# A graph convolution whose pools are opened once, and whose table is loaded or made in parts between the first block's products

## The chip, the core and the metric

The kernel runs on one core of a Trainium2 chip. The metric is the device time of one execution in microseconds (us). The five engines each work through a queue of their own in order: PE (TensorE, matrix products), DVE (VectorE), ACT (ScalarE), POOL (GpSimd, which here only issues the row gathers) and SP (SyncE, which issues nearly all other transfers). They meet through semaphores. SBUF is the working memory on the chip, with 128 partitions, and PSUM is where matrix products land. DRAM stands for the memory outside the core's SBUF and PSUM.

## What is computed

A graph of 12,500 nodes with 128 features and 200,000 edges, sorted by destination, goes through an attention layer (the first half of the time, which the change leaves alone) and then through three graph convolutions with batch norm. The part that matters:

```python
def _gcn_conv(x, W, b, src, dst, norm, num_nodes):
    h = x @ W
    msg = h[src] * norm[:, None]
    out = jax.ops.segment_sum(msg, dst, num_segments=num_nodes)
    return out + b
def _batch_norm(x, gamma, beta):
    mean = jnp.mean(x, axis=0)
    var = jnp.mean((x - mean) ** 2, axis=0)
    return (x - mean) * jax.lax.rsqrt(var + EPS) * gamma + beta
...
src, dst, norm = _gcn_norm(edge_index, n)        # dinv[src] * dinv[dst], with self loops
h = _gcn_conv(x, W1, b1, src, dst, norm, n)      # 128 -> 256
h = _batch_norm(jax.nn.relu(h), g1, beta1)
h = _gcn_conv(h, W2, b2, src, dst, norm, n)      # 256 -> 128
h = _batch_norm(jax.nn.relu(h), g2, beta2)
h = _gcn_conv(h, W3, b3, src, dst, norm, n)      # 128 -> 128
return _batch_norm(h, g3, beta3)
```

## The kernel before

**The data of a convolution.** A convolution sums, for each destination node, rows of a table `t_d[i]` (12,544 rows of 128 floats in DRAM, already scaled by `dinv`). The same table stands in SBUF as `hs`, 98 slices of 128 rows (6.4 MB). The destinations are cut into 106 tiles of `TN` = 118 nodes. An edge can go two ways. For each pair of a tile and a slice there are 13 slots, so most edges are served by a matrix product that picks rows out of `hs`. The others, at most 768 a tile, are gathered row by row from `t_d[i]` by POOL.

**`take(b, m)`** (L1211 to L1229) serves block `b`, which is nine tiles; there are 12 blocks. It goes through the 98 slices in seven parts of `SG` = 14 slices. For each part it loads the indices `gi` (L1215), VectorE turns them into a one-hot `go` (L1221, four slices at a time), PE multiplies it with the slices of `hs` (L1224), ScalarE copies the product to `stage` (L1226), and two transfers store it to a block `m` in DRAM (L1228).

**`reduce(b, m)`** (L1231) takes the tiles of a block one by one. Each needs the block's `m` complete: it is read back in another order as `mr` (L1245), and a tile has 20 matmul instructions over `mr` (L1253) and 12 over the gathered `rows` (L1255). The gathers of a tile are six POOL instructions on line 148 (the helper `gather`), into the pool `ga` with five buffers. `finish` (L1150) begins a tile with its own rows `tg` (L1154, L1159) and ends three tiles with the scaling by `dinv` (L1163) and the function `use`.

**The order.** The parts of `take(b)` and the tiles of `reduce(b - 1)` alternate, so block 0 is taken alone, and the last block, with seven tiles, is reduced alone. After the last tile the statistics of the batch norm (L1275, L1280) give a scale and a shift; `affine` (L1277) and `through` (L1288) put them into the next weights. Then `transform` (L1301) makes the next table: groups of `NG` = 4 slices, on PE (L1312), two passes on VectorE (L1315, L1316, the latter writing `hs`), and a store to `t_d[i]` (L1318). For the second convolution it also loads half of the features, `hb`, from DRAM (L1307). The first convolution finds its table in `t_d[0]` and loads `hs` in one transfer:

```python
                nc.sync.dma_start(hs, rows_of(t_d[0], 0, NS))            # L1324
                ...
                conv(t_d[0], use1)
                sr = s.enter_context(tc.tile_pool(name="sr", bufs=3))
                ps = s.enter_context(tc.tile_pool(name="ps", bufs=2, space=PSUM))
                ...
                transform(sr, ps, [hb_d], wa, row, t_d[1])
```

After the third convolution an output loop loads `x1` (L1376), multiplies by the scale (L1381), adds (L1384, L1388) and stores (L1389), four slices at a time.

**Pools.** `conv_slots` opens its pools anew for each convolution and closes them at its end. `sr` (three buffers of each of its tiles: `hb`, `og`, `x1`, `yg`) and a PSUM pool for `transform` are opened after that. The order of instructions within each engine's queue isn't the order of the program text: a scheduler in the framework sorts them at build time, by the program's order and by when it reckons an instruction can start. It tracks which parts of a tile or a table an instruction reads and writes. `conv_rows` stands beside `conv_slots` for graphs with too many gathered edges a tile; this input takes `conv_slots`.

Of the kernel before, what the change touches and what calls it, by code (L numbers as in the profile page):

```python
# [8 lines left out]
FP = mybir.dt.float32  # L9
BF = mybir.dt.bfloat16  # L10
# [7 lines left out]
P = 128  # L18
D = 128
# [29 lines left out]
def tile_gnn(ctx: ExitStack, tc: tile.TileContext, x, src, dst, ea, wqkvT, weT, w1, w2, w3, par, out):  # L49
# [26 lines left out]
    def groups(n, g):  # L76
        return [(a, min(g, n - a)) for a in range(0, n, g)]
# [580 lines left out]
    def fast():  # L658
# [505 lines left out]
                                    op=ALU.mult)  # L1164
            use(wk, t0, n, zt[:, :n * TN], ps)

        def conv_rows(table, use):

            with ExitStack() as s:
                ew = s.enter_context(tc.tile_pool(name="ew", bufs=1))  # L1170
                srcA = ew.tile([P, NTT, JJ], I32, name="srcA")
                dlA = ew.tile([P, NTT, JJ], BF, name="dlA")
                nc.sync.dma_start(srcA, sw_d.rearrange("t (p j) -> p t j", j=JJ))
                nc.sync.dma_start(dlA, dlb_d.rearrange("t (p j) -> p t j", j=JJ))
                ga = s.enter_context(tc.tile_pool(name="ga", bufs=3))
                wk = s.enter_context(tc.tile_pool(name="wk", bufs=2))
                ps = s.enter_context(tc.tile_pool(name="ps", bufs=2, space=PSUM))
                for t0, n in groups(NTT, GN):
                    zp = ps.tile([P, GN, TN], FP, name="zp")

                    def add(i):
                        rows = ga.tile([P, JJ, D], FP, name="rows")
                        for j in range(JJ):
                            gather(rows[:, j, :], table, srcA[:, t0 + i, j:j + 1])
                        oh = wk.tile([P, JJ, TN], FP, name="oh")
                        one_hot(oh, dlA[:, t0 + i, :])
                        for j in range(JJ):
                            nc.tensor.matmul(zp[:, i, :], rows[:, j, :], oh[:, j, :], start=False, stop=(j == JJ - 1))

                    for _ in finish(wk, table, t0, n, zp, use, ps, add):  # L1190
                        pass

        def conv_slots(table, use):

            with ExitStack() as s:
                tb = s.enter_context(tc.tile_pool(name="tb", bufs=1, space=PSUM))
                nums = tb.tile([P, TN], FP, name="nums")
                nc.vector.tensor_copy(nums, iota_f[:, :TN])  # L1200
                blocks = s.enter_context(tc.tile_pool(name="blocks", bufs=3, space=DRAM))
                gy = s.enter_context(tc.tile_pool(name="gy", bufs=3))
                gx = s.enter_context(tc.tile_pool(name="gx", bufs=3))
                sg = s.enter_context(tc.tile_pool(name="sg", bufs=2))
                mt = s.enter_context(tc.tile_pool(name="mt", bufs=3))
                ga = s.enter_context(tc.tile_pool(name="ga", bufs=5))
                wk = s.enter_context(tc.tile_pool(name="wk", bufs=2))
                ps = s.enter_context(tc.tile_pool(name="ps", bufs=2, space=PSUM))
                TS = TB * SB

                def take(b, m):  # L1211
                    for g in range(NS // SG):
                        stage = sg.tile([TS, SG, D], FP, name="stage")
                        gi = gy.tile([P, TB, SG * SB], U8, name="gi")
                        nc.sync.dma_start(gi.rearrange("p t k -> p (t k)"),  # L1215
                                          gi_d[b, g].rearrange("t k -> (t k)").unsqueeze(0)
                                          .to_broadcast([P, TS * SG]))
                        gv = gi.rearrange("p t (s k) -> p s t k", k=SB)
                        for a, n in groups(SG, 4):
                            go = gx.tile([P, 4, TB, SB], FP, name="go")  # L1220
                            nc.vector.tensor_scalar(go[:, :n], gv[:, a:a + n], iota_q, None, op0=ALU.is_equal)  # L1221
                            gp = ps.tile([TS, 4, D], FP, name="gp")
                            for i in range(n):
                                nc.tensor.matmul(gp[:, i, :], go[:, i].rearrange("p t k -> p (t k)"),  # L1224
                                                 hs[:, g * SG + a + i, :], start=True, stop=True)
                            nc.scalar.copy(stage[:, a:a + n, :], gp[:, :n, :])  # L1226
                        for x, y in ((0, 112), (112, TS)):
                            nc.sync.dma_start(m[x:y, g * SG:(g + 1) * SG, :], stage[x:y])  # L1228
                        yield  # L1229
# [31 lines left out]
                for b in range(NBK + 1):  # L1261
# [8 lines left out]
                    for _ in tiles:  # L1270
                        pass

        def stats(st, h, t0, n):
            w = min(n * TN, N - t0 * TN)
            nc.vector.bn_stats(st[:, t0 // GN, :], h[:, :w])  # L1275
# [11 lines left out]

        def through(pool, ps, abs_, ws):  # L1288

            br = ps.tile([P, D], FP, name="br")  # L1290
            wa = []
            for k, (ab, w) in enumerate(zip(abs_, ws)):
                wk_ = pool.tile([P, D], FP, name=f"wa{k}")
# [4 lines left out]
            nc.vector.tensor_copy(row, br)  # L1298
            return wa, row

        def transform(sr, ps, more, wa, row, table):  # L1301

            for s0, n in groups(NS, NG):
                parts = [big[:, s0 * P:(s0 + n) * P]]
                for h in more:
                    hb = sr.tile([P, NG * P], FP, name="hb")
                    nc.sync.dma_start(hb[:, :n * P], h[:, s0 * P:(s0 + n) * P])  # L1307
                    parts.append(hb)
                tp = ps.tile([P, NG, D], FP, name="tp")
                for i in range(n):  # L1310
                    for k, (h, w) in enumerate(zip(parts, wa)):
                        nc.tensor.matmul(tp[:, i, :], h[:, i * P:(i + 1) * P], w, start=(k == 0),  # L1312
# [6 lines left out]

        def convolutions(conv):  # L1320
            with ExitStack() as s:
                once = s.enter_context(tc.tile_pool(name="once", bufs=1))
                st = [once.tile([P, NST, 6], FP, name=f"st{k}") for k in range(2)]
                nc.sync.dma_start(hs, rows_of(t_d[0], 0, NS))  # L1324

                def use1(wk, t0, n, zt, ps):
                    a, b = t0 * TN, (t0 + n) * TN
                    hx = wk.tile([P, GN * TN], FP, name="hx")
                    for k, h in enumerate((big[:, a:b], hx[:, :b - a])):
                        hq = ps.tile([P, GN * TN], FP, name="hq")  # L1330
                        nc.tensor.matmul(hq[:, :n * TN], w1s[:, k * D:(k + 1) * D], zt, start=True, stop=True)
                        nc.scalar.activation(h, hq[:, :n * TN], AF.Relu, bias=pars[:, k:k + 1])
                        stats(st[k], h, t0, n)
                    nc.sync.dma_start(hb_d[:, a:b], hx[:, :b - a])

                conv(t_d[0], use1)
                sr = s.enter_context(tc.tile_pool(name="sr", bufs=3))
                ps = s.enter_context(tc.tile_pool(name="ps", bufs=2, space=PSUM))
                abs_ = [affine(once, st[k], pars[:, 2 + k:3 + k], pars[:, 4 + k:5 + k], k) for k in range(2)]
                wa, row = through(once, ps, abs_, [w2s[:, k] for k in range(2)])  # L1340
                transform(sr, ps, [hb_d], wa, row, t_d[1])

            with ExitStack() as s:
                once = s.enter_context(tc.tile_pool(name="once", bufs=1))
                st = once.tile([P, NST, 6], FP, name="st")

                def use2(wk, t0, n, zt, ps):
                    h = big[:, t0 * TN:(t0 + n) * TN]
                    nc.scalar.activation(h, zt, AF.Relu, bias=pars[:, 6:7])
                    stats(st, h, t0, n)  # L1350

                conv(t_d[1], use2)
                sr = s.enter_context(tc.tile_pool(name="sr", bufs=3))
                ps = s.enter_context(tc.tile_pool(name="ps", bufs=2, space=PSUM))
                ab = affine(once, st, pars[:, 7:8], pars[:, 8:9], 0)
                wa, row = through(once, ps, [ab], [w3s])
                transform(sr, ps, [], wa, row, t_d[2])

            with ExitStack() as s:
                once = s.enter_context(tc.tile_pool(name="once", bufs=1))  # L1360
                st = once.tile([P, NST, 6], FP, name="st")

                def use3(wk, t0, n, zt, ps):
                    h = big[:, t0 * TN:(t0 + n) * TN]
                    nc.scalar.activation(h, zt, AF.Identity, bias=pars[:, 9:10])
                    stats(st, h, t0, n)

                conv(t_d[2], use3)
                sr = s.enter_context(tc.tile_pool(name="sr", bufs=3))
                ps = s.enter_context(tc.tile_pool(name="ps", bufs=2, space=PSUM))  # L1370
                ab = affine(once, st, pars[:, 10:11], pars[:, 11:12], 0)
                wa, row = through(once, ps, [ab], [ident])
                for s0, n in groups(NS, NG):
                    full = min(n, N // P - s0)
# [1 line left out]
                    nc.sync.dma_start(x1[:, :full, :], rows_of(x1_d, s0, full))  # L1376
                    if full < n:
                        nc.sync.dma_start(x1[:N % P, full, :], x1_d[(s0 + full) * P:N, :])
                    yp = ps.tile([P, NG, D], FP, name="yp")
                    for i in range(n):  # L1380
                        nc.tensor.matmul(yp[:, i, :], big[:, (s0 + i) * P:(s0 + i + 1) * P], wa[0], start=True, stop=True)  # L1381
                    for r, m in ((P, slice(0, full)), (N % P, slice(full, n))):
# [67 lines left out]
```

## Time and profile before

| | |
|---|---|
| median of 3 runs | 7293.77 us (7284.83 to 7306.85) |
| the profiled execution | 6154.56 us, of which its span 6152.8 us |
| mean granted TensorE clock in it | 0.796 of full speed |
| busy: PE, DVE, ACT, POOL | 4406.0, 3396.2, 1011.7, 4084.2 us |
| attention layer and preparation | 0 to 2970 us |
| three convolutions | 2970 to 6093 us |
| output loop | 6093 to 6153 us |

The median and the profiled execution are different executions of the same kernel, and the profiled one is 1139 us shorter. Durations below are those of the profiled one. In the profile's rows, "L1224 PE MATMUL gp<-hs,go x7056" is the group of matmul instructions of line 1224 that read `hs` and `go` and write `gp`; each product of float32 data is two matmul instructions. PEld is the load of the stationary operand, which overlaps PE. SPq is SP's queue of transfers. In the timeline a row gives the start, the duration, the engine, the line, and in brackets how long the engine had been idle and what it waited for last; rows of equal instructions that follow each other are merged.

### The profile page before, as it was taken

How to read it: one execution, taken by the hardware profiler on the slowest of the kernel's cores; microseconds unless marked ns; L12 is line 12 of the kernel's file. 1: busy time of each engine (PE TensorE's matmuls, PEld its weight loads, DVE VectorE, ACT ScalarE, POOL GpSimd, SP SyncE). 2: the span in 40 equal slices, each digit the busy share in tenths (PEclk: the TensorE clock that was granted, in tenths of full speed). 3: DMA queues.
4: the chain of work that ended last, by engine and by line, in shares of the span. 5: the costliest groups of instructions: out<-in, count | busy, mean ns of one | idle time of the engine just before them, and what ended most of it. 6: DMA issues, size and time to landing. Idle time of an engine off the chain costs nothing. (4 is left out here: it accounts for less than half of the span.)

```text
span 6152.8 us, 80384 instructions
## 1 busy us (share of the span) xinstructions
PE 4406.0 (72%) x28564; PEld 4115.5 (67%) x28564; DVE 3396.2 (55%) x5972; ACT 1011.7 (16%) x2374; POOL 4084.2 (66%) x3617
## 2 busy tenths in 40 slices
PE   6676666666666665767487787877787787778777
PEld 2666655555566665666377777777777776777777
DVE  7566688887876677655243343353343344434344
ACT  3111111110111111111112122111121211112120
POOL 0777788888888888777266566636666664666663
PEclk9677766666676776767788888898888888888888
DMA  6555544433444444454588888878888887888888
GB/s 188 152 143 138 137 112 106 113 103 109 105 128 120 122 112 112 131 132 114 150 214 216 218 216 218 213 209 217 219 216 221 213 211 204 219 219 219 221 215 209
DMA packets 607714, 1051.07 MB, mean 171 GB/s; under 512 B 191227, under 2 KB 418491, under 8 KB 607201
## 3 DMA queue, kind: packets, MB, share of 16 engines
q1 hardware_dynamic: 464311, 695.85, 41.5%
q0 software_dynamic: 142608, 348.39, 23.9%
q8 instruction: 232, 3.80, 0.3%
q14 instruction: 175, 1.43, 0.1%
q10 hardware_dynamic: 388, 1.60, 0.1%
HBM read 773.19 MB, written 272.26 MB: 170 GB/s over the span
## 5 line engine op out<-in xcount | busy, mean ns | idle before, releaser
L148 POOL DMA_INDIRECT rows<-t_d,srcO x1908 | 1827.6, 958 | 1329.2 <-issue 560.2
L148 POOL DMA_INDIRECT kv<-kv_d,srcA x1696 | 2252.3, 1328 | 536.7 <-issue 484.3
L1249 DVE TENSOR_TENSOR oh<-nums,dlS 128x1888 f32<-128x1888 f32 x318 | 674.3, 2121 | 1527.2 <-PE zp L1255 1517.9
L1253 PE MATMUL zp<-oh,mr 128*128 128x118 f32 x6360 | 966.6, 319 | 567.5 <-DMA mr<-m 440.4
L1253 PEld LDWEIGHTS zp<-oh,mr 128*128 128x128 f32 x6360 | 925.5, 233 | 586.4 <-DMA mr<-m 348.7
L1019 PE MATMUL qe<-qt,oht 128*128 128x128 f32 x3392 | 841.4, 415 | 247.3 <-DVE kv L1020 110.7
L1224 PE MATMUL gp<-hs,go 128*117 128x128 f32 x7056 | 891.8, 281 | 125.8 <-DVE go L1221 69.8
L1019 PEld LDWEIGHTS qe<-qt,oht 128*128 128x128 f32 x3392 | 767.1, 310 | 289.7 <-issue 166.8
L1224 PEld LDWEIGHTS gp<-hs,go 128*117 128x117 f32 x7056 | 831.9, 184 | 165.1 <-issue 117.1
L1226 ACT COPY stage<-gp 117x512 f32<-117x512 f32 x1008 | 521.8, 532 | 1375.0 <-PE gp L1224 936.8
L1020 DVE TENSOR_TENSOR kv<-qe,kv 128x512 f32<-128x512 f32 x424 | 289.4, 685 | 678.8 <-DMA kv<-kv_d,srcA 536.8
L1089 PE MATMUL acc<-vals,oh 128*118 128x137 f32 x3392 | 539.8, 329 | 150.5 <-DVE vals L1082 150.0
L1089 PEld LDWEIGHTS acc<-vals,oh 128*118 128x118 f32 x3392 | 522.1, 225 | 171.6 <-DVE vals L1082 171.3
L1221 DVE TENSOR_SCALAR go<-gi,iota_q 128x468 f32<-128x468 uint8 x1008 | 427.8, 456 | 224.5 <-DMA gi<-gi_d 111.8
L1255 PE MATMUL zp<-oh,rows 128*128 128x118 f32 x3816 | 513.2, 288 | 0.2 <-DMA rows<-t_d,srcO 0.2
L1255 PEld LDWEIGHTS zp<-oh,rows 128*128 128x128 f32 x3816 | 492.2, 206 | 0.4 <-DMA rows<-t_d,srcO 0.4
L1058 PE MATMUL ends<-ident,mg 128*8 128x128 f32 x212 | 53.0, 343 | 344.4 <-DVE mg L1053 305.6
L1082 DVE TENSOR_TENSOR vals<-kv,vals 128x2048 f32<-128x2048 f32 x106 | 242.3, 2286 | 27.2 <-ACT vals L1081 26.8
L1058 PEld LDWEIGHTS ends<-ident,mg 128*8 128x8 f32 x212 | 11.7, 96 | 366.1 <-DVE mg L1053 298.8
L1023 DVE TENSOR_REDUCE sc<-kv 128x128 f32<-128x2048 f32 x106 | 240.8, 2272 | 0.0
L677 DVE TENSOR_TENSOR oh<-iota_f,dlA 128x1888 f32<-128x1888 f32 x106 | 224.0, 2113 | 5.0 <-PE acc L1089 5.0
L1036 PE MATMUL sm<-wbd,et 128*128 128x32 f32 x848 | 167.8, 351 | 45.0 <-DVE mg L1075 37.7
(242 smaller groups left out, 3648.1 us busy)
## 6 DMA issues: line engine op xcount, KB each, us to landing
m<-stage SPq DMA_DIRECT2D x252, 784.0 KB
mr<-m SPq DMA_DIRECT2D x318, 560.0 KB
dw_b<-dlb_d SPq DMA_DIRECT2D x106, 512.0 KB
gi<-gi_d SPq DMA_DIRECT2D x252, 204.8 KB
rows<-t_d,srcO POOLq DMA_INDIRECT x1908
kv<-kv_d,srcA POOLq DMA_INDIRECT x1696
ebx<-in_edge_attr_dram SPq DMA_DIRECT2D x106, 256.0 KB
mr<-m SPq DMA_DIRECT2D x318, 75.0 KB
```

The lines of the kernel that those rows point to most:

```text
L148: nc.gpsimd.indirect_dma_start(out=o, out_offset=None, in_=table[:, :], in_offset=bass.IndirectOffsetOnAxis(ap=idx, axis=0))
L1019: nc.tensor.matmul(qe[:, k, :], ohv[:, :, j + k], qt, start=True, stop=True)
L1020: nc.vector.tensor_tensor(qk[:, j:j + 4, :], qe, qk[:, j:j + 4, :], op=ALU.mult)
L1023: nc.vector.tensor_reduce(sc.rearrange("p h j -> p j h"), qk.rearrange("p j (h c) -> p j h c", h=H), AX.X, ALU.add)
L1082: nc.vector.tensor_tensor(vh[:, :, :, :C], kv[:, :, D:].rearrange("p j (h c) -> p j h c", h=H), vh[:, :, :, C:].to_broadcast([P, JJ, H, C] ...
L1089: nc.tensor.matmul(acc, oh[:, j, :], va[:, j, :], start=(j == 0), stop=(j == JJ - 1))
L1221: nc.vector.tensor_scalar(go[:, :n], gv[:, a:a + n], iota_q, None, op0=ALU.is_equal)
L1224: nc.tensor.matmul(gp[:, i, :], go[:, i].rearrange("p t k -> p (t k)"), hs[:, g * SG + a + i, :], start=True, stop=True)
L1226: nc.scalar.copy(stage[:, a:a + n, :], gp[:, :n, :])
L1249: nc.vector.tensor_tensor(oh, nums.unsqueeze(1).to_broadcast(sh), dlS[:, t, :].unsqueeze(2).to_broadcast(sh), op=ALU.is_equal)
L1253: nc.tensor.matmul(zp[:, i, :], mr[:q, j, :], oh[:q, j, :], start=False, stop=False)
L1255: nc.tensor.matmul(zp[:, i, :], rows[:, j, :], oh[:, RC + j, :], start=False, stop=(j == JO - 1))
```

## The change

The pools of a convolution are opened once for all three, by `conv_slots(s)`, which returns the PSUM pool and a function `run(table, use, ready)`. Before the products of part `g` in block 0, `take` now calls `ready(g)`. In the first convolution `ready` is `load`, one of seven loads of `hs`; in the second and third it is `transform` for the 14 slices of the part, in groups of 4, 4, 4 and 2. All products that go through PSUM outside `take` and `reduce` share one name, `bank`. `ga` has four buffers instead of five, and `sr`, now open throughout, two instead of three. `nums` is filled once. The core of the diff:

```diff
+        def pools(s, *names):
+            return [s.enter_context(tc.tile_pool(name=n, bufs=b)) for n, b in names]
+
+        def bank(ps):
+            return ps.tile([P, NG * D], FP, name="bank")
...
-        def conv_slots(table, use):
-            with ExitStack() as s:
-                tb = s.enter_context(tc.tile_pool(name="tb", bufs=1, space=PSUM))
-                nums = tb.tile([P, TN], FP, name="nums")
-                nc.vector.tensor_copy(nums, iota_f[:, :TN])
-                blocks = s.enter_context(tc.tile_pool(name="blocks", bufs=3, space=DRAM))
-                gy = s.enter_context(tc.tile_pool(name="gy", bufs=3))
...
-                ga = s.enter_context(tc.tile_pool(name="ga", bufs=5))
...
+        def conv_slots(s):
+            gy, gx, sg, mt, ga, wk = pools(s, ("gy", 3), ("gx", 3), ("sg", 2), ("mt", 3), ("ga", 4), ("wk", 2))
+            blocks = s.enter_context(tc.tile_pool(name="blocks", bufs=3, space=DRAM))
+            tb = s.enter_context(tc.tile_pool(name="tb", bufs=1, space=PSUM))
+            ps = s.enter_context(tc.tile_pool(name="ps", bufs=2, space=PSUM))
+            nums = tb.tile([P, TN], FP, name="nums")
+            nc.vector.tensor_copy(nums, iota_f[:, :TN])
+            TS = TB * SB
+
+            def run(table, use, ready):
                 def take(b, m):
                     for g in range(NS // SG):
+                        if b == 0:
+                            ready(g)
                         stage = sg.tile([TS, SG, D], FP, name="stage")
...
+            return ps, run
+
...
-        def transform(sr, ps, more, wa, row, table):
-
-            for s0, n in groups(NS, NG):
+        def transform(sr, ps, more, wa, row, table, g):
+
+
+            for s0, n in [(g * SG + a, n) for a, n in groups(SG, NG)]:
...
         def convolutions(conv):
             with ExitStack() as s:
-                once = s.enter_context(tc.tile_pool(name="once", bufs=1))
+                once, sr = pools(s, ("once", 1), ("sr", 2))
+                ps, run = conv(s)
                 st = [once.tile([P, NST, 6], FP, name=f"st{k}") for k in range(2)]
-                nc.sync.dma_start(hs, rows_of(t_d[0], 0, NS))
+
+                def load(g):
+                    nc.sync.dma_start(hs[:, g * SG:(g + 1) * SG, :], rows_of(t_d[0], g * SG, SG))
...
+                run(t_d[0], use1, load)
                 abs_ = [affine(once, st[k], pars[:, 2 + k:3 + k], pars[:, 4 + k:5 + k], k) for k in range(2)]
                 wa, row = through(once, ps, abs_, [w2s[:, k] for k in range(2)])
-                transform(sr, ps, [hb_d], wa, row, t_d[1])
...
+                run(t_d[1], then(AF.Relu, 6), lambda g: transform(sr, ps, [hb_d], wa, row, t_d[1], g))
+                ab = affine(once, st[0], pars[:, 7:8], pars[:, 8:9], 0)
+                wa3, row3 = through(once, ps, [ab], [w3s])
+                run(t_d[2], then(AF.Identity, 9), lambda g: transform(sr, ps, [], wa3, row3, t_d[2], g))
+                ab = affine(once, st[0], pars[:, 10:11], pars[:, 11:12], 0)
                 wa, row = through(once, ps, [ab], [ident])
```

`then(func, b)` is the old `use2` and `use3` in one function.

## The prediction

> **What bounds the kernel now.** I read the time of each stretch first, because the change touches only the three graph convolutions and mainly their starts. The stretches below are cut at the first product over the exchanged blocks (L1253) and at the end of each convolution; columns are length, busy time and instruction count of each engine, granted clock, DMA share and GB/s.
>
> ```profile
> core 0: us, PE busy (x) PEld busy (x) DVE busy (x) ACT busy (x) POOL busy (x), PEclk, DMA share, GB/s
> 2970.00:3066.00 96.00, 38.13 (x255) 35.84 (x256) 19.80 (x40) 17.50 (x35) 28.50 (x30) 0.68 0.83 201
> 3066.00:4030.00 964.00, 768.41 (x5847) 740.82 (x5845) 388.32 (x512) 194.16 (x374) 579.27 (x606) 0.88 0.81 215
> 4030.00:4145.00 115.00, 84.15 (x652) 80.66 (x653) 60.24 (x114) 18.05 (x37) 29.25 (x30) 0.88 0.75 218
> 4145.00:5072.00 927.00, 735.39 (x5703) 718.73 (x5701) 367.29 (x474) 173.85 (x338) 580.50 (x606) 0.89 0.84 216
> 5072.00:5168.00 96.00, 63.58 (x451) 59.09 (x452) 53.32 (x103) 17.85 (x36) 29.27 (x30) 0.84 0.68 201
> ...
> 6093.00:6153.00 60.00, 33.30 (x199) 30.06 (x198) 37.08 (x66) 0.59 (x2) 0.00 (x0) 0.81 0.71 202
> ```
>
> The long stretches are set by PE (80%) together with DMA (81 to 84%). The three starts, 96 + 115 + 96 = 307 us, are where no engine and no transfer is full: PE is busy 40 to 73%. The last 60 us are the output. The timeline shows what the starts are made of.
>
> ```profile
> 2972.42 5.96 SPq L1324 DMA_DIRECT2D hs<-t_d  x1
> 2978.43 24.46 SPq L1215 DMA_DIRECT2D gi<-gi_d  x3
> 3007.92 3.74 PE L1224 MATMUL gp<-hs,go 128*117 128x128 f32 x16 [49.90 <-DMA tg<-t_d]
> ...
> 4115.97 5.04 PE L1224 MATMUL gp<-hs,go 128*117 128x128 f32 x28 [8.41 <-DVE go L1221]
> ...
> 4121.19 3.42 PE L1224 MATMUL gp<-hs,go 128*117 128x128 f32 x28 [0.18 <-ACT stage L1226]
> ```
>
> The load of the whole table (6.4 MB) is issued at 2972.4, and the first product runs 35 us later. In the other starts the new table is made first, and then block 0 is taken with waits of 8.4 us for its indices, after which 28 matmuls take 5.0 instead of 3.4 us.
>
> ```profile
> 6102.77 0.50 SPq L1376 DMA_DIRECT2D x<-x_d  x1
> ...
> 6105.85 0.69 DVE L1384 TENSOR_TENSOR x<-x,row 128x512 f32<-128x512 f32 x1 [2.11 <-DMA x<-x_d]
> ```
>
> In the output VectorE waits for a load issued 3.1 us earlier: with three buffers this loop is limited by latency.
>
> **The first convolution's start.** One load becomes seven, each before the part that reads it. Part 0 with its indices is 0.92 + 0.2 MB; at the 288 to 291 GB/s of the windows from 2980 to 3010 that is 3.9 us, and with 3 us to land the first product comes near 2980, 28 us sooner. It can't all be kept, as the bytes remain: up to the first block product the queues move the table 6.4, nine index loads 1.8, nine stores of `m` 7.4, four tiles of gathers 1.6 and about 1 of `tg` and `db`, 18.2 MB, or 63 us at 290 GB/s, against 93.7 us now (2972.4 to 3066.1). So between -31 and -10 (if the index waits stay and the stores queue behind the loads): I take -23. Here a rule speaks against the change: the Trainium skill (DMA: Bandwidth & Descriptors, section Bandwidth) wants transfers of 1 MiB or more for 75% of peak, and each part is 0.92 MB. By the rule the load would lose a quarter, 22 us becoming 29, and the saving 7. But in the row nearest, the 256 KB loads and stores of the transform (4040 to 4080), the queues moved 262 to 279 GB/s, 4 to 9% below the large load: 1 to 2 us. I go by the row.
>
> **The second start.** It is counted from the end of the batch-norm constants (4035.5) to the first block product (4145.1): 109.6 us. The transform's work is not removed but put between the parts. Per part it has 14 x 4 matmul instructions of 0.11 us, 6.2 us, and the part's own product 3.4: 9.6 us if PE never waits. If PE's queue stays strictly in order, the product waits for the last two VectorE passes (2 x 0.69 us), and two `hb` buffers instead of three leave about 1.6 us of load time open (a load lands 3.1 us after its issue: 4077.19 to 4080.26): 12.6. Seven parts: 67 to 88 us. Two parts of block 1 and the trip of `m` through DRAM follow as now, 8 + 5. Sum 80 to 101, and the DMA floor is near (21.5 MB at 275 GB/s: 78). Saving 9 to 30; I take 17. The waits of 8.4 us are hidden by transform matmuls; without that cover they cost 17 again.
>
> **The third start.** From 5075.7 to 5168.4: 92.7 us. VectorE ran 10.00 of 10 us in the transform (5080 to 5100). 98 blocks in parts of 14 make 28 groups instead of 25 (4, 4, 4, 2): 7 x (6 x 0.69 + 2 x 0.41) = 35 us, and 7 x 1.7 for the index comparisons (0.45 x 3 + 0.34): 47 us if VectorE stays full; 7 x 9.3 = 65 if each product of 3.4 us with its first following transform holds VectorE up. With 13 as above 60 to 78 (DMA floor 17 MB: 62). Saving 15 to 33; I take 21.
>
> Behind both: the gathers (L148) need the whole table, so POOL's queue of 24 waits for the last transform's store instead of running during block 0. The first tile then needs 2.5 + 6 x 1.25 + 2 = 12 us, and its first use is at least 14 us after that store (last part, `m` out and back, two parts of block 1); later tiles need 7.5 us each against 9 us of use. I cost it at nothing; uncovered, up to 12 us twice. Only L1255 and, behind it on PE, everything else would wait. Opening pools once takes out two copies of `nums` (0.3 us each): nothing.
>
> **Gather buffers, five to four.** I replayed the gathers with the recorded times of their users: six issues of 1.25 us, started when the buffer comes free.
>
> ```profile
> L148 POOL DMA_INDIRECT rows<-t_d,srcO x1908 | 1827.6, 958 | 1329.2 <-issue 560.2
> ```
>
> Between the convolution's ends nothing changes: with four buffers the gathers end over 14 us before use. In the last seven tiles PE takes 3.8 us per tile, and gathers 7.5. The least lead over a convolution is now 5.9 us in the first and 2.5 us in the third, where PE just touches it (a wait of 0.2 at 5067.2); it falls by 7.5 us to -1.6 and -5.0, and with 2.3 us for landing PE waits 3.9 and 7.3; for the second, with records missing, the mean, 5.6. Sum +17 (0 if the tail's matmuls run slower).
>
> **Buffers of `sr`, three to two.** In the output one loop is load 3.6 us (mean of 3.1, 4.3, 3.0, 4.6, 3.1), two VectorE passes 1.5, two issues 0.8: 5.9 us. Over three buffers it gives 2.0 us a group, which is the trace (49.7 us for 25). Over two it gives 2.95, or 2.65 if the load falls to 3.0 us in a less crowded queue: +16 to +23, with +8 if it lands in 2.3. I take +19.
>
> **Sum.** -23 - 17 - 21 + 17 + 19 = -25 us, against the profiled execution's 6154.6. The runs shown take 7293.8, 1139 more, and no view says where. If their matmuls run slower, the tails outlast the gathers (+17 goes to 0) and the starts keep their hidden waits: about -45. Between -25 and -45 I take -35: 7259.
>
> **Rivals.**
>
> (a) Slower: the buffers given up outweigh the overlap. SP's queue is in order; a store of `m` waits on it for ScalarE (the longest SP wait of the profile, 1338.8 us in 249), and behind it now stand `hb` loads, `t_d` stores and the next part's loads. If each part costs such a wait again (4 to 5 us), the second start saves nothing, the third 8, the first 10: -18 + 36 = +18, and with late gathers up to +30. It decides once the starts save less than 36 us. 7319. For it speaks that DMA is near its floor in two starts; against it that SP already interleaves stores and loads of the transform every 1.8 us without holding up PE (8.7 to 9.8 of 10 us busy).
>
> (b) Faster: the parts overlap to the DMA and engine floors: -31 - 30 - 33, the output +8, the tails 0: -86. 7208.
>
> (c) It doesn't do what it says: `hs` could be guarded as a whole, so that part g+1 waits for the products of part g and saves nothing: +36, 7330. Against it: VectorE wrote `hs` without a pause while stores of earlier slices of it were in flight.
>
> **How the numbers follow.** Forecast 0.60 (its own range 7234 to 7284), (b) 0.15, (a) 0.20, (c) 0.05. A measurement of this kernel can tell about 0.3%, 22 us, from no change. Of the forecast's chance 0.42 lies beyond that and 0.18 within; (b) is beyond it; (a) gives 0.07 within and 0.13 slower; (c) slower. Faster 0.57, same 0.25, slower 0.18. The range runs from below (b), 7200, to just short of (a), 7318.
>
> **What would show it.** First `gp` product within 10 us of the first `hs` load, and starts of about 71, 93 and 72 us; transform matmuls between the products of block 0; no wait of 8 us for `gi` there; POOL's first gather after the last `t_d` store and `rows` waits of PE only in the tails, 4 to 7 us each; the output near 68 us with `x` loads ending VectorE's waits. Wrong would be: starts as long as now, a long wait of PE on `rows` in the first block, or a change of the stretches between (964 and 927 us) by more than 10 us, which I count as unchanged.

## The result, and the profile after

The changed kernel takes 7273.74 us in the median of 12 runs (7233.97 to 7308.87), the kernel before 7272.05 us in 12 runs beside it (7244.70 to 7309.31). The ratio is 0.9995, with an interval of 0.9971 to 1.0020: between 21 us less and 15 us more. That is no change. The range on record holds the time; the saving of 35 us that it was built on did not come.

One thing has to be known to read the numbers below. In five groups of timed runs the kernel before took 7272 us (this comparison, with the runs shown at first among them) and 7282 us (one later group), but 6162 to 6165 us in the three others, each of them on another chip. The profiled execution of before, 6154.6 us, belongs to the second kind, and the profile of after that comes with the result (span 7258.4 us, 7260.22 us for the execution) to the first. I call the first kind a chip that holds PE back, for reasons shown next. Two profiles from different kinds can't be subtracted, so I ran both kernels again side by side.

The first extract holds the stretches of the changed kernel in the profile that came with the result, with the columns named in the prediction: the first start, the first long stretch, the third start, the third long stretch, and the output (the second start, from 4464 to 4606, took 142 us).

```profile
3090.00:3177.00 87.00, 42.23 (x250) 39.73 (x251) 19.35 (x39) 17.74 (x35) 22.91 (x24) 0.66 0.88 212
3177.00:4463.00 1286.00, 869.66 (x5853) 815.12 (x5852) 395.23 (x533) 192.36 (x376) 585.81 (x612) 0.82 0.62 163
...
5843.00:5943.00 100.00, 63.95 (x452) 60.41 (x453) 46.08 (x95) 18.04 (x35) 22.80 (x24) 0.80 0.62 177
5943.00:7186.00 1243.00, 841.27 (x5704) 810.77 (x5703) 379.44 (x483) 178.88 (x339) 585.16 (x612) 0.78 0.62 161
7186.00:7259.00 73.00, 43.55 (x198) 38.14 (x198) 34.66 (x56) 0.00 (x0) 0.00 (x0) 0.60 0.61 170
```

The long stretches, which the change leaves alone, have as many instructions as before and last 1286 and 1243 us, against 964 and 925 us. The transfers are at 62%, so they don't set this; VectorE and POOL are busy for as long as before. The same kernel on a chip of the other kind (span 6160.0 us) gives this:

```profile
2979.00:3056.00 77.00, 39.72 (x252) 37.91 (x253) 19.63 (x39) 17.55 (x35) 22.94 (x24) 0.70 0.97 240
3056.00:4037.00 981.00, 772.43 (x5855) 743.55 (x5853) 398.45 (x538) 194.12 (x376) 584.51 (x612) 0.88 0.82 213
4037.00:4154.00 117.00, 90.89 (x677) 85.39 (x676) 50.14 (x97) 20.31 (x40) 10.38 (x11) 0.91 0.66 201
...
5083.00:5155.00 72.00, 58.84 (x452) 55.94 (x453) 45.51 (x95) 17.94 (x36) 19.23 (x20) 0.91 0.85 240
...
6087.00:6160.00 73.00, 45.36 (x198) 40.02 (x198) 34.38 (x53) 0.00 (x0) 0.00 (x0) 0.59 0.61 170
```

The 1098 us between these two spans of one kernel lie in the three long stretches (924 us), in the attention layer (111 us) and in the starts (63 us); the output is equal. So the 1139 us for which no view had a place in the prediction lie between executions in different places, and not in the kernel. I speak of chips; each chip was seen in one session only, so that chip and session can't be told apart. What it looks like from inside is in PE's timeline of a long stretch on the first kind of chip:

```profile
5795.19 0.61 PE L1260 MATMUL zp<-oh,mr 128*128 128x118 f32 x2
5796.85 0.26 PE L1260 MATMUL zp<-oh,mr 128*128 128x118 f32 x1 [1.05 <-issue]
5797.58 0.45 PE L1260 MATMUL zp<-oh,mr 128*128 128x118 f32 x2 [0.47 <-issue]
5798.98 0.36 PE L1260 MATMUL zp<-oh,mr 128*128 128x118 f32 x1 [0.95 <-issue]
...
5802.51 1.00 PE L1260 MATMUL zp<-oh,mr 127*128 127x118 f32 x4 [1.74 <-issue]
```

PE starts single matmuls 0.7 us or a multiple of it apart, and in the pauses waits for nothing that the profile shows ("issue"). The page's groups of the same profile, for the gathers and for the products of `take` (busy time, mean ns of one, idle time ahead and what ended it):

```profile
L148 POOL DMA_INDIRECT rows<-t_d,srcO x1908 | 1824.0, 956 | 2299.4 <-PE zp L1159 716.3
...
L1231 PE MATMUL gp<-hs,go 128*117 128x128 f32 x7056 | 1068.0, 309 | 656.8 <-issue 478.1
```

The gathers cost what they did (956 against 958 ns), but POOL now idles 2299 instead of 1329 us, first behind PE; PE's idle time ahead of the products of `take` went from 126 to 657 us, 478 of it "issue".

Of the steps that were to show in the profile of after, these did, the first only in kind: the first `gp` product comes 14.1 us after the first load of `hs` (35 us before; I had said within 10); transform matmuls stand between the products of block 0; on the chip that holds PE back, PE has no wait for `rows` at a convolution's end. And the output loop waits for its loads:

```profile
7191.03 1.87 SPq L1369 DMA_DIRECT2D x<-x_d  x2
...
7195.20 0.69 DVE L1377 TENSOR_TENSOR x<-x,row 128x512 f32<-128x512 f32 x1 [4.65 <-DMA x<-x_d]
```

VectorE waits 4.65 us, where the row of before had 2.11. Over the whole loop its waits for `x` sum to 29 us, against 11 us before: that is the 18 us by which the loop got longer.

### The profile page after: what moved, and what is told of

It reads as the page before. It is cut to its first block, busy times and chain, and to the rows that moved or that the text cites. A ratio compares the mean times of both kernels' runs of the same rounds, so it can differ in the third digit from the quotient of the medians.

```text
span 7258.4 us, 80385 instructions
## 1 busy us (share of the span) xinstructions
PE 4759.2 (66%) x28564; PEld 4404.5 (61%) x28564; DVE 3413.5 (47%) x5982; ACT 1018.4 (14%) x2374; POOL 4050.7 (56%) x3617
## 5 line engine op out<-in xcount | busy, mean ns | idle before, releaser
L148 POOL DMA_INDIRECT kv<-kv_d,srcA x1696 | 2222.5, 1310 | 682.2 <-issue 491.5
L1231 PE MATMUL gp<-hs,go 128*117 128x128 f32 x7056 | 1068.0, 309 | 656.8 <-issue 478.1
L1260 PE MATMUL zp<-oh,mr 128*128 128x118 f32 x6360 | 1063.7, 339 | 603.9 <-DMA mr<-m 319.1
L1231 PEld LDWEIGHTS gp<-hs,go 128*117 128x117 f32 x7056 | 967.8, 209 | 739.1 <-issue 572.9
L1260 PEld LDWEIGHTS zp<-oh,mr 128*128 128x128 f32 x6360 | 1020.9, 252 | 623.1 <-issue 363.2
L1262 PE MATMUL zp<-oh,rows 128*128 128x118 f32 x3816 | 538.4, 292 | 48.2 <-issue 47.5
L1262 PEld LDWEIGHTS zp<-oh,rows 128*128 128x128 f32 x3816 | 510.5, 210 | 61.6 <-issue 60.9
```

Of the source, the lines that this page charges most:

```text
L148: nc.gpsimd.indirect_dma_start(out=o, out_offset=None, in_=table[:, :], in_offset=bass.IndirectOffsetOnAxis(ap=idx, axis=0))
L1260: nc.tensor.matmul(zp[:, i, :], mr[:q, j, :], oh[:q, j, :], start=False, stop=False)
L1262: nc.tensor.matmul(zp[:, i, :], rows[:, j, :], oh[:, RC + j, :], start=False, stop=(j == JO - 1))
```

## The experiments

A stage in what follows is measured as in the prediction: a start runs from the first load of `hs`, or from the batch-norm constants, to the first product over `mr`; a long stretch from there to the next constants; the output from the last constants to the end. Ratios are to the kernel before on the same chip.

I set four theories against each other. Buffers: what the starts save is paid again by the buffers given up (`ga`, and the two of `sr`), as in rival (a). Order: putting the parts of the transform between the products costs by itself, since a product waits for the VectorE passes ahead of it. No effect: rival (c). Held back (H): on a chip that holds PE back, filled gaps are given back.

### Both kernels side by side, and the buffers given back or taken away

`base_again` and `after_again` are the two kernels unchanged, for a pair of profiles from one chip.

> The kernel before, unchanged, profiled once more. Theory H (held back): PE's matmuls are held back in the long stretches whatever the order of the work, and the first profile of before (6154.6 us) caught an execution without that. H expects a time near 7270 us, long stretches near 1250 us instead of 927 to 964, single matmuls about 0.7 us apart in places, and starts near 96, 115 and 96 us or some us longer. Theory C (cancelled): the long stretches of the two kernels differ because of the change, and gains at the starts are given back in them. C expects long stretches of 930 to 970 us again and a time near 6154.

> The changed kernel once more. H: near 7270 us or, in an execution that isn't held back, near 6130, since the starts are then shorter by some 50 to 60 us and tails and output longer by some 30. C: near 7260, with long stretches of 1240 to 1290 us as in its first profile.

`after_r5` is the changed kernel again, timed in five rounds.

> The changed kernel, timed in five rounds beside the kernel before on one chip where PE isn't held back. Cancelled (the sum of the stretches: first start -15, second +6, third -19, later stretches +9, output +18): ratio 1.000 within 0.2%. If its one run there was a slow one, the ratio is 0.994 to 0.996 as the sum on record had it.

The single runs gave 6165.47 us (before) and 6164.78 us (after). Of the two recorded theories, H had put the changed kernel near 6130 us or 7270 and C near 7260; neither came, though the kernel before did what C said. The timed comparison gave 6167.24 us against 6165.23 us, ratio 1.0003 (0.9995 to 1.0012): on this kind of chip as well there is no change. By stage, in us:

| term | prediction | `after_again` less `base_again` | `after_r5` less `base_again` |
|---|---|---|---|
| first start | -23 | 77.1 - 92.2 = -15.1 | 76.9 - 92.2 = -15.3 |
| second start | -17 | 119.0 - 112.9 = +6.1 | 117.0 - 112.9 = +4.1 |
| third start | -21 | 72.9 - 92.4 = -19.5 | 71.9 - 92.4 = -20.5 |
| long stretches (tails) | +17 | +9.3 | +8.6 |
| output | +19 | 72.9 - 54.7 = +18.2 | 73.1 - 54.7 = +18.4 |
| sum | -25 | -1.0 | -4.7 |

The spans of the first pair differ by 0.7 us, so its table is complete. "No effect" falls: the first and third start are 15 and 20 us shorter. What remains of the gain is eaten, and the second start has the wrong sign.

`a_full` gives the buffers back to the changed kernel. To make room, `hb` and `x1` share one name, and `og` and `yg` another; they are never needed together.

```diff
-("ga", 4)
+("ga", 5)
-once, sr = pools(s, ("once", 1), ("sr", 2))
+once, sr = pools(s, ("once", 1), ("sr", 3))
-hb = sr.tile(..., name="hb")     # and x1
+hb = sr.tile(..., name="sin")    # both
-og = sr.tile(..., name="og")     # and yg
+og = sr.tile(..., name="sout")   # both
```

> The changed kernel with what it gave up put back: five gather buffers and three buffers in sr, made possible by one name for the tiles that are loaded and one for those that are stored. My sum counted 17 us for the gather buffers and 19 us for sr, so 36 us less than the changed kernel, ratio to before near 0.993 in both the sum and C. H: the output gets 15 to 20 us shorter in its window, the tails don't, and the whole is within 0.3% of the kernel before.

`b_ga4_sr2` is the kernel before with the buffers taken away and nothing else:

```diff
-ga = s.enter_context(tc.tile_pool(name="ga", bufs=5))
+ga = s.enter_context(tc.tile_pool(name="ga", bufs=4))
-sr = s.enter_context(tc.tile_pool(name="sr", bufs=3))   # three times
+sr = s.enter_context(tc.tile_pool(name="sr", bufs=2))
```

> The kernel before with four gather buffers and two of sr, the costs alone. The sum: +17 in the tails and +19 in the output, 36 us, ratio 1.005. H: the tails outlast the gathers, so only the output's 15 to 20 us, ratio 1.002 or 1.003.

`a_full`: 6115.44 us, ratio 0.9922 (0.9908 to 0.9937), 48 us faster. `b_ga4_sr2`: 6205.81 us, ratio 1.0072 (1.0057 to 1.0087), 42 us slower, where 36 were expected. The buffers alone are worth about as much as the overlap alone. In `b_ga4_sr2` the output took 71.6 us (+17), the long stretches 20.9 more in sum, the second start 121.5 (+8.6). In `a_full` the stages lie as follows (three starts, and the output):

```profile
2976.00:3054.00 78.00, 38.70 (x254) 36.82 (x255) 19.45 (x40) 17.84 (x35) 29.01 (x30) 0.73 0.99 242
4029.00:4133.00 104.00, 84.05 (x677) 80.84 (x676) 50.83 (x97) 20.83 (x40) 12.27 (x13) 0.94 0.78 234
5054.00:5129.00 75.00, 61.25 (x457) 58.64 (x458) 46.78 (x93) 18.33 (x36) 21.39 (x22) 0.87 0.83 233
6059.00:6114.00 55.00, 33.66 (x198) 30.14 (x197) 34.01 (x53) 0.00 (x0) 0.00 (x0) 0.78 0.78 221
```

The first and third start are as in the changed kernel, the output is back at 55 us, and the second start has fallen from 117 to 104. The theory of the buffers holds on this chip.

### Which buffer: loads, gathers, stores

`a_sin3` gives back only the third buffer of the loads; the gathers keep four and the stores two:

```diff
-once, sr = pools(s, ("once", 1), ("sr", 2))
+once, si, sr = pools(s, ("once", 1), ("si", 3), ("sr", 2))   # si: hb and x1; sr: og and yg
```

> The changed kernel with three buffers instead of two for the loaded tiles (hb and x1, which share them); stored tiles two, gathers four. If the two load buffers are what lost the second start and the output (theory L), the second start falls from 119 us to about 104, as with all buffers put back, the output from 73 to about 55, tails stay; 33 us less than the changed kernel, ratio to before near 0.995. If it was the gather buffers or a later start of the gathers that cost it (theory G), the time stays at 6165, ratio 1.000.

`a_ga5` gives back only the fifth gather buffer (the shared names as in `a_full`, two buffers each).

> The changed kernel with five gather buffers; loaded and stored tiles two each as in the change (hb and x1 share a name, og and yg share one, to make room). L: only the tails' 9 us come back, PE no longer waits for rows in the tails, second start stays near 119 and output near 73; ratio near 0.9985. G: 30 us or more come back, ratio below 0.996.

`a_best` has five gather buffers, four for the loads and three for the stores (`("ga", 5)`, `("si", 4)`, `("sr", 3)`).

> Five gather buffers, four for the loaded tiles, three for the stored ones. L, if the loads are still late at three buffers (PE waited 1.2 to 2.7 us for them in each part): second start near 95 us instead of 104, output near 50 instead of 55, ratio near 0.990. If three were enough: as with three, 0.992.

| kernel | us | ratio | second start | long stretches | output |
|---|---|---|---|---|---|
| `after_r5` | 6167.24 | 1.0003 (0.9995 to 1.0012) | 117.0 | 2841.6 | 73.1 |
| `a_ga5` | 6148.27 | 0.9977 (0.9967 to 0.9987) | 119.3 | 2824.2 | 73.2 |
| `a_sin3` | 6129.12 | 0.9952 (0.9935 to 0.9969) | 102.0 | 2840.3 | 59.3 |
| `a_full` | 6115.44 | 0.9922 (0.9908 to 0.9937) | 103.8 | 2826.1 | 54.9 |
| `a_best` | 6112.50 | 0.9918 (0.9901 to 0.9936) | 110.7 | 2827.1 | 50.7 |

The fifth gather buffer takes 17 us out of the long stretches, where I had expected 9, and leaves the rest alone. The third load buffer takes 15 us out of the second start and 14 out of the output. The two don't touch each other's stages. A fourth load buffer shortens the output by another 4 us, but the second start isn't better (110.7 where I had expected 95). In its trace PE still waits 13.4 us for the loads there, 5.6 of them at once (12.0 in `a_full`), and the granted clock is 0.88, against 0.94. Why the loads stay late was not found, and `a_best` can't be told from `a_full` in time.

The waits that the fifth buffer removes look like this in PE's timeline of `after_again`, here at the end of the second convolution:

```profile
5062.60 0.78 PE L1262 MATMUL zp<-oh,rows 128*128 128x118 f32 x2 [2.63 <-DMA rows<-t_d,srcO]
```

They sum, with the small ones, to 1.2, 3.2 and 4.2 us in the three convolutions. I had worked out 3.9, 5.6 and 7.3. They are about half of what the buffer is worth: the tails, from the last product of `take` to the constants, sum to 162.2 us in `base_again`, 176.2 in `after_again` and 160.0 in `a_ga5`. What else lengthens them with four buffers was not found.

### The first start alone

`b_load7` is the kernel before with only the first convolution's load cut into seven, each ahead of its part of block 0:

```diff
 for g in range(NS // SG):
+    if b == 0 and ready:
+        ready(g)
...
-nc.sync.dma_start(hs, rows_of(t_d[0], 0, NS))
+def load(g):
+    nc.sync.dma_start(hs[:, g * SG:(g + 1) * SG, :], rows_of(t_d[0], g * SG, SG))
```

> The kernel before with only the first convolution's table loaded in seven parts between the products of block 0; all pools and buffers as before. The first start falls from 92 us to 77 as it did in the change, the rest stays: 15 us, ratio near 0.9976. If the later stretches take it back, 1.000.

6143.58 us, ratio 0.9965 (0.9952 to 0.9979); the first start took 78.2 us, all other stages were those of before. So this part acts by itself, and gives 14 us of the start. Why not 23 is in PE's timeline of the first start in `after_again`:

```profile
2992.69 5.34 PE L1231 MATMUL gp<-hs,go 128*117 128x128 f32 x28 [27.91 <-issue]
...
3025.32 9.54 PE L1231 MATMUL gp<-hs,go 128*117 128x128 f32 x56 [11.04 <-DVE go L1228]
...
3050.05 5.67 PE L1231 MATMUL gp<-hs,go 128*117 128x128 f32 x28 [7.88 <-DVE go L1228]
```

The products start 22 us earlier than before, and not 28. Then they wait 11 and 8 us for the one-hots, that is for the index loads behind them (8.2 and 8.4 us in `base_again`), so that from the first product to the first product over `mr` 63 us pass, against 56. Where the six us at the beginning are is in SP's queue, with two stretches of the transfers behind it:

```profile
2978.63 6.61 SPq L1337 DMA_DIRECT2D hs<-t_d  x1
2985.29 0.92 SPq L1222 DMA_DIRECT2D gi<-gi_d  x1
...
2983.00:2988.00 5.00, 0.00 (x0) 0.00 (x0) 0.43 (x1) 0.00 (x0) 2.16 (x3) 0.50 1.47 101
2988.00:2993.00 5.00, 0.31 (x1) 0.34 (x2) 1.08 (x3) 0.00 (x0) 1.61 (x2) 0.50 1.10 296
```

The first load holds SP's queue for 6.6 us, though it has a seventh of the bytes (6.0 in `base_again`), and the indices of part 0 are issued only then. Until 2988 little moves. After that the parts come at 290 to 303 GB/s (2988 to 3003), as fast as the one large load before. The share of 0.97 to 0.99 in the start's rows above isn't full queues throughout: in `after_again` a mean of 0.96 is made of shares of up to 1.47 at the beginning and of 0.53 to 0.87 in seven of the sixteen stretches of 5 us. So its 237 GB/s are bytes over time, and no rate of full queues.

### The second start: loads or order

`a_nohb` leaves out the loads of `hb`; the second half of the second convolution's weights is multiplied with the first half of the features.

```diff
-hb = sr.tile([P, NG * P], FP, name="hb")
-nc.sync.dma_start(hb[:, :n * P], h[:, s0 * P:(s0 + n) * P])
-parts.append(hb)
+parts.append(big[:, s0 * P:(s0 + n) * P])
```

> The changed kernel without the loads of hb: the second transform multiplies the first half of the features twice instead, so its values are others and its matmuls and stores the same. If the loads of hb through two buffers are what made the second start 119 us (L), it falls by the waits of about 3 us a part and the matmuls at half clock after them, to 90 to 95. If the order of the queues (products of block 0 between the transform's) is what costs it (O), it stays above 112.

`a_ahead` is `a_full` with the table made one part ahead of the products: parts 0 and 1 before the first product, and part g + 1 at g.

```diff
-ready(g)
+for k in range(2 if g == 0 else 1):
+    if g + k + (g > 0) < NS // SG:
+        ready(g + k + (g > 0))
```

> All buffers put back (five gather, three of loads and stores), and the table made one part ahead: parts 0 and 1 before the first products, then part g+2's making stands before the products of part g+1. If PE's strict order still costs a part its VectorE latency (my 12.6 us a part), the second start falls from 104 to below 97 and the third from 75 to below 70; ratio 0.990. If the scheduler had hidden that already, 0.992 as without.

Without the loads the second start took 85.8 us, against 119.0, and the kernel 6120.01 us (one run). With a part ahead it took 102.5 us, against 103.8 in `a_full`: nothing. "Order" falls: the same number of instructions (677 of PE), parts and products alternating as before, fits in 86 us once the loads are gone. How the loads cost is in PE's timeline of `after_again`:

```profile
4047.85 1.60 PE L1231 MATMUL gp<-hs,go 128*117 128x128 f32 x10
4052.34 0.80 PE L1322 MATMUL bank<-wa,hb 128*128 128x128 f32 x2 [2.89 <-DMA hb<-hb_d]
4052.93 0.63 PE L1322 MATMUL bank<-wa,big 128*128 128x128 f32 x2
...
4060.00 0.39 PE L1322 MATMUL bank<-wa,big 128*128 128x128 f32 x2
...
4068.84 0.79 PE L1322 MATMUL bank<-wa,hb 128*128 128x128 f32 x2 [3.06 <-DMA hb<-hb_d]
```

Such a wait comes once a part, six times in all: 2.89, 3.06, 2.60, 2.36, 3.61 and 2.42 us. Around four of them (2.89, 3.06, 3.61 and 2.42) two matmuls take 0.63 us instead of 0.39 for some microseconds, so a wait then costs more than its length. The granted clock of stretches around the first, the third and the fifth wait shows when (PE's busy time, clock, DMA share and GB/s):

```profile
4048.22:4051.63 3.41, 1.12 (x9) 1.00 0.91 268
4051.63:4055.05 3.42, 2.71 (x12) 0.50 0.38 121
...
4082.35:4085.77 3.42, 1.72 (x15) 1.00 0.51 166
4085.77:4089.18 3.41, 3.10 (x24) 1.00 0.60 185
...
4109.66:4113.07 3.41, 0.90 (x8) 1.00 0.45 164
4113.07:4116.48 3.41, 3.37 (x17) 0.50 0.16 40
```

The clock changes only on a grid of 3.41 us, and it halves after a stretch of the grid in which PE was busy for little: 1.12, 0.48, 0.90 and 1.17 us before the four drops, 1.72 and 1.93 us at the waits of 2.60 and 2.36, which lie across two stretches. The wait of 3.61 us ends 0.9 us before its drop.

Part of each wait is SP's queue, in which the loads of a part stand behind two stores of the table:

```profile
4046.44 2.16 SPq L1328 DMA_DIRECT2D t_d<-hs  x2
4048.70 0.95 SPq L1317 DMA_DIRECT2D hb<-hb_d  x2
```

PE's last product over `hb` before them had ended at 4046.8, so both buffers had been free for about 2 us when their loads were issued. A part takes 15.0 us (the mean of the five intervals from 4049.45, where the first wait begins, to 4124.58). With three load buffers, in `a_full`, the wait of the same place is this:

```profile
4062.11 0.49 PE L1322 MATMUL bank<-wa,sin 128*128 128x128 f32 x2 [1.69 <-DMA sin<-hb_d]
```

There the six waits are 1.25, 1.69, 2.65, 1.29, 1.17 and 3.03 us, and a part takes 12.1 us. What is left to `a_nohb` (18 us) is these waits and 6.4 MB less to transfer; the two weren't taken apart.

`a_ahead` also came out at 6131.01 us, ratio 0.9945 (0.9931 to 0.9959), some 14 us behind `a_full`; its first start was 5 us longer (82.9), its long stretches 9. The cause of the latter stays open.

### The chip that holds PE back

`a_full_2` is `a_full` again, on a chip of the first kind.

> The changed kernel with all buffers put back, once more in a session of its own, to see it on a chip where PE is held back if this one is (the kernel before near 7270 us there, near 6164 elsewhere). Elsewhere: ratio 0.992 as before. Where PE is held back: H expects 1.000 within 0.3%, since waits that are filled with matmuls are given back by matmuls held back later; if holding back only stretches what is there, the 50 us stay, ratio 0.993.

7265.30 us (22 runs) against 7282.18 (27 runs), ratio 0.9982 (0.9965 to 0.9999): 13 us by the ratio, 17 by the medians. On the other kind of chip the same kernel saved 48 us, ratio 0.9922 (0.9908 to 0.9937); the intervals don't meet. So this part of H holds as a fact: the same filled gaps and buffers are worth less there, 1 to 26 us by the interval, against 39 to 57. In its profile the starts take 94.2, 128.5 and 103.9 us, the long stretches 1282.5, 1237.2 and 1241.7, the output 55.0. A profile of before on such a chip would say where the rest goes; I have none, and how it is given back stays open.

## Where the prediction was right and where it failed

**First start, -23.** Right in kind, too large: -15. The prediction's upper case ("if the index waits stay and the stores queue behind the loads", -10) was nearer than the value taken. Two terms were mis-sized. The first product was to come 28 us sooner and came 22 sooner: the 6 us that the first load holds SP's queue, which stand in the line shown there (5.96), were put at nothing. And the waits for the indices stayed, 18.9 us against 16.6, and one of 3.9 us behind the stores of `stage` was added, so that 7 us of the gain were lost again. From the rule weighed there (the Trainium skill, DMA: Bandwidth & Descriptors, section Bandwidth) I had estimated a loss of 7 us, which leaves 16; from the row taken instead 1 to 2. The 14 of `b_load7` are nearer to the rule's figure, but by luck: once they flow, the parts come as fast as the large load.

**Second start, -17.** This is the step that failed, in sign: +6 and +4. The working gave a part 9.6 us "if PE never waits" and 12.6 with the VectorE passes and "about 1.6 us of load time open", and I took a value between. A part took 15.0 us: seven make 105, and with the 13 us after them that is the 118 measured. The runs show the passes hidden (`a_ahead`, `a_nohb`) and the loads not: 2.4 to 3.6 us a part instead of 1.6. The slower PE after four of the six waits, 17 us at half clock from 4051.6 to 4130.1, was in no term of the sum. In `base_again`, with three buffers and the loads in a stage of their own, such waits were 1.0, 1.0 and 2.1 us.

**Third start, -21.** Right: -19.5 and -20.5. It has no loads in its transform.

**Gathers, +17.** Nearly right in size, not in the way: the tails got 14 us longer, the long stretches as a whole 9. The waits are where I put them, at the ends of the convolutions, but with 9 us in all they are only a part of it. The clause that they go to nothing "if their matmuls run slower" is borne out: on the chip that holds PE back the changed kernel has none there.

**Output, +19.** Right: +18.2, the same on both kinds of chip (73 us). 14 of it are the latency of the loads over two buffers (`a_sin3`); the other 4 came back with the third buffer of the stores (`a_full`).

**The sum, and the step to the runs shown.** On the scale of the profile, -25 became -1 to -5, and 23 of the difference are the second start, 8 the first, less 8 for the long stretches. The prediction then went from -25 to -35, because in slower runs the starts would "keep their hidden waits" while the tails are spared. The tails were spared. Whether the starts kept more there can't be read without a profile of before, but the whole saving didn't grow: that of `a_full` shrank from 48 to 13 us on such a chip. That the range holds the time, and that 7259 lies only 15 us off it, is luck: the kernel before came out 22 us faster in the twelve runs than in the three on which the 7259 rests. The result, -21 to +15, lies between the forecast and rival (a), whose mechanism the runs show in part: the starts save 28.5 us, below its limit of 36, and the buffers cost 27.5 instead of 36, so that they cancel the overlap and don't outweigh it; its waits in SP's queue are seen in the second start, while the third saved what was forecast.

**Better than both** is `a_full`: 0.9922 on one kind of chip, 0.9982 on the other, the latter with an interval that ends at 0.9999.

## What to carry to other kernels

When pools are merged so that stages overlap, count the buffers of each tile in both of its places: a tile with two buffers that is loaded between products cost PE a wait of 2.4 to 3.6 us each time, and a third, under a name shared with a tile of another stage, took it to 1.2 to 3.0. A transfer floor (64 us at 290 GB/s for the first start) says little while the loads wait for each other in one queue: here 77 us were measured. And before a sum is made on a profile, ask whether the profile's time is that of the runs: here they differed by 15%, and a saving of 48 us on one chip was 13 on the other.

## What the runs showed of the hardware

The same kernel takes 6164 us on some chips and 7272 on others, and in a profile of the second kind PE starts many matmuls at multiples of 0.7 us with nothing to wait for. The granted clock tells little of it: 0.82 and 0.78 in the long stretches, against 0.88 and 0.90, 7 to 13% lower, where the stretches last 31 to 33% longer. What holds PE back was not found.

PE's granted clock takes two values, 0.5 and 1, and changes only on a grid of 3.41 us. In four traces (`before`, `after_again`, `a_full` and `after`) each of the 672 stretches of this grid at full clock in which PE was busy for less than 1.25 us was followed by half clock; of the 2420 with 3 us and more, 33 were. None of the 1835 at half clock with less than 2.75 us was followed by full clock. So half clock followed a wait of 2.42 us that left PE 1.17 us busy in its stretch, and did not follow one of 2.60 us that lay across two. The Trainium skill (TensorE: Matmul & The Clock Gate, section Why this matters for your kernels) advises to keep PE's pauses below about 3 us for its clock's sake; two pauses below that, of 2.42 and 2.89 us, were enough here.
